# Moving one shift and one scaling of a layer norm between two matmul groups in a two-layer graph kernel

## The chip, the cores and the metric

The kernel runs on one core of one Trainium2 chip. The metric is device microseconds of one execution. A core has TensorE (matmuls, PE in the profile, with its weight loads as PEld), VectorE (DVE), ScalarE (ACT), GpSimd (POOL) and SyncE (SP), which here issues all DMA transfers.

## The reference

64 graphs of 256 nodes with 512 features, in two layers, all float32:

```python
# layer 0
deg = sum(adj, -1);  agg = (adj @ x) / max(deg, 1e-6)
x = layernorm(x + relu(concat([x, agg]) @ W.T))
# layer 1
q, k = split(x @ Wqk);  v = x @ Wv
agg = adj @ (k * mask)
w = mask * sum(q * agg, -1) / sqrt(512)
x = layernorm(x + softmax(w, over the nodes) * v)
```

The layer norm takes mean and variance over the 512 features of a node.

## The kernel before, in words

Graphs are worked on in 32 pairs. The main loop (`for j in range(NP)`) does layer 0 of pair j, and interleaves with its last third layer 1 of pair j-1, so that one round of the loop finishes one pair. A "graph" below is one of the two of a pair, k = 0 or 1; each has its 256 nodes in two tiles of 128, t = 0 and 1.

The matrix products are rearranged. Adjacency is applied after the feature weights, and the query and key weights are multiplied together once at the start. Each product of a 256x512 activation with a 512x512 weight is done in the Strassen-Winograd way: seven products P1 to P7 of blocks instead of eight, with sums of blocks prepared ahead. P1, P2, P3 and P5 are split once more in the same way inside (`inner`, L340), so each is four steps: `first_two`, `second`, `third`, `last_two`. P4, P6 and P7 are plain (`pairs`, L732, four units: two graphs with two halves each). `gather` (L405 on) is the product with the adjacency, with letters a to g.

The eight PSUM banks are used in four pairs. An `inner` product has a work bank (one half `lo`, one half `hi`) and a pair of target banks. Its steps follow this scheme: a matmul into `lo`, then ScalarE copies `lo` into a target bank, then the next step's matmul overwrites `lo`. In `third` ScalarE copies `lo` into both halves of the second target bank (128x512) and `hi` into a small tile, `fifth` (128x256). P5 of layer 0 and P3 of both layers share one work bank, P1 and P2 another. So a matmul of the next step or of the next product can start only when ScalarE has made its copy.

The order on every engine is the order in which the Python program emits instructions. The strings such as `run("p l p l p l", ...)` (L910) fix the order of TensorE by hand: each letter takes the next unit of a product. There p are the units of P4 of layer 1 and l the steps of P3 of layer 1 (`open1`); the last l and P3's end run in the next round (L795), between the first steps i of P1 and k of P5 of layer 0.

All other VectorE and ScalarE work is put into chains of steps (`queue`, L137): "norm" for the norm of layer 0, "softmax", "adds", "finish" for the norm of layer 1, "mask", "degrees", "sums". After most units `tick` (L152) goes through the chains by rank and emits a step when a planner's clock says so: the clock of TensorE goes forward by 0.43 or 0.86 us a matmul (`mm`, L174), each step has a cost and an estimated time at which its predecessor on another engine is done (L148). `flush` emits what is left of named chains. The planner decides only the order; on the chip, semaphores decide when.

The norm chain of a graph (`norm_of`, L478, called by `norm0`, L525) is: mean on VectorE (tile `less`), two squares with their sums on ScalarE (`junk`, `var`), the factor on ScalarE (`rstd`), the shift on VectorE (`shift` = `less` * `rstd`), and two scalings on ScalarE (`own` = `own` * `rstd` + `shift`), one for each tile. After the last one, a second chain of the same name holds two VectorE transposes (`turn`). A DMA then puts the pieces in place for the transposed activation of layer 1 (`places`, L798). Ahead of it, `send_scores` (L573) sends the scores of the pair before to DRAM and back, spread over all partitions for the softmax.

The scores themselves come from `dot` (L694): VectorE multiplies a bank of P4 (`u`) with the aggregated tile and sums it. The dot product of graph 0 follows the second unit p, that of graph 1 the fourth.

Of the kernel before, what the change touches and what calls it, by code (L numbers as in the profile page):

```python
# [94 lines left out]
def resnorm_kernel(  # L95
# [15 lines left out]
    NT, NF, NA = N // P, F // P, A // P  # L111
    H, HF = NF // 2, F // 2
    NP = B // 2
# [16 lines left out]
    clock, chains, shared, quiet = [0.0], [], [1.0], [False]  # L130
# [13 lines left out]
    def step(chain):  # L144
        _, name, ready, steps = chain
        eng, work = steps.popleft()
        work()
        ready[0] = eng.free + (0.4 if eng is not vec else 0.7 if name == "norm" and len(steps) == NT else 2.2 if name == "finish" or name == "norm" and steady else 1.4) if steps and steps[0][0] is not eng else 0.0  # L148
        if not steps:
            chains.remove(chain)  # L150
# [10 lines left out]
    def flush(*names):  # L161
        while True:
            c = next((c for c in chains if not names or c[1] in names), None)
            if not c:
                return
            step(c)

    def run(order, **units):
        for name in order.split():
            units[name].pop(0)()  # L170
# [31 lines left out]
    def load_xT(j, home=None):  # L202
        Xs[j] = Side(pool, "xT", S1, home)
        for k in range(2):
            first(Xs[j].a[:, k].rearrange("p h e t n -> p (h e) (t n)"),
                   x_t[2 * j + k].rearrange("(c p) n -> p c n", p=P))
# [78 lines left out]
    def fourth_sums(X, ks=(1, 0)):  # L285

        for k in ks:
            k = slice(k, k + 1)
            gp.tensor_sub(X.block(S4, k), X.block(A12, k), X.block(S2, k))
        if ks[-1] == 0:  # L290
            inner_sums(X, gp, 2)
# [27 lines left out]
    def mask_adj(j):  # L319
        def mask(k, t):  # L320
            act.activation(adjs[j][:, k, t], adjs[j][:, k, t], AF.Copy,
                           scale=mask_sb[:, 2 * j + k, t:t + 1])
        queue(4, "mask", *[(act, lambda k=k, t=t: mask(k, t)) for k in range(2) for t in range(NT)])

    def degrees(j):
        deg = small.tile([P, 2, NT], F32, name="deg")
        rdeg = rdegs[j] = small.tile([P, 2, NT], F32, name="rdeg")
        r = rows.pop(j)

        def degree(k, t):  # L330
            act.activation(r[:, k, t], r[:, k, t], AF.Copy, accum_out=deg[:, k, t:t + 1])

        def invert():
            vec.tensor_scalar(rdeg, deg, DEG_EPS, None, op0=OP.max)
            vec.reciprocal(rdeg, rdeg)
        queue(2, "degrees", *[(act, lambda k=k, t=t: degree(k, t)) for k in range(2) for t in range(NT)],
              (vec, invert))


    def inner(p, X, sides, w, q, done=lambda fifth: None):  # L340

        n, block = {"P1": (0, A11), "P2": (1, A12), "P5": (2, S1), "P3": (0, S4)}[p]
        b = sides[p]
        s = lambda r: X.i[:, r, n]
        lo, hi = w[:, :HF], w[:, HF:]
        fifth = []

        def first_two():
            mm(hi, s(0), b["T1"], start=True)
            mm(lo, X.chunk(block, 0, 0), b["B11"])  # L350
            act.copy(q[0][:, :HF], lo)
            tick()

        def second():
            mm(lo, s(1), b["T2"])
            act.copy(q[0][:, HF:], lo)
            tick()

        def third():
            mm(lo, s(2), b["T3"])  # L360
            act.copy(q[1].rearrange("p (h f) -> p h f", h=2),
                           lo[:, None, :].to_broadcast([P, 2, HF]))
            fifth.append(small.tile([P, HF], F32, name="fifth", bufs=3))
            act.copy(fifth[0], hi)
            mm(q[0][:, :HF], X.chunk(block, 0, 1), b["B21"])
            tick()

        def last_two():
            mm(q[1][:, :HF], X.chunk(block, 1, 1), b["T4"])
            mm(q[0][:, HF:], s(3), b["B22"])  # L370
            if p in ("P1", "P5"):
                for k in range(2):
                    vec.tensor_add(q[k][:, HF:], q[k][:, HF:], fifth[0])
            done(fifth[0])
            tick()
        return [first_two, second, third, last_two]
# [15 lines left out]
    def sums_T(val, later=None, n=3):  # L392

        b11, b12, b21, b22 = (val[:, :, t, h * HF:(h + 1) * HF] for t in range(NT) for h in range(2))
        tv = pool.tile([P, 4, 2, HF], F32, name="tv")
        t1, t2, t3, t4 = (tv[:, r] for r in range(4))
        vec.tensor_sub(t1, b12, b11)
        rest = [lambda args=args: vec.tensor_sub(*args) for args in ((t2, b22, t1), (t3, b22, b12), (t4, b21, t2))]
        for do in rest[:n]:
            do()  # L400
        if n < len(rest):
            later.extend(rest[n:])
        return {"B11": b11, "B21": b21, "B22": b22, "T1": t1, "T2": t2, "T3": t3, "T4": t4}
# [328 lines left out]
    def pairs(ps, X, slot, b, done):  # L732
        return outer(ps, 0, X, slot, b, done) + outer(ps, 1, X, slot, b, done)
# [23 lines left out]
    open1 = None  # L757
    early = []

    for j in range(NP):  # L760
        X = Xs.pop(j)
        if j == 2:
            steady.append(True)
        flush("finish")
        owns[j] = pool.tile([P, 2, NT, F], F32, name="own", bufs=3)
        if j > 0:
# [11 lines left out]
        p, q = pairs(u, X, S2, W0["T2"], a6), pairs(u, X, S3, W0["T3"], a7)  # L778
        r, s = inner("P3", X, W0, pw[1], y, a3), pairs(u, X, A22, W0["T4"], a4)
        if j == 0:  # L780
            run("i k i k i k i k", i=i, k=k)
            flush("degrees")
            load_rows(1)
        elif j == 1:
            early.append(a1)
            run("k i k m k i k", i=early[0], k=k, m=m)
            fourth_sums(X, [1])
            run("m p p", m=m, p=p)
            fourth_sums(X, [0])
            run("p p m", m=m, p=p)  # L790
            load_x(1)
        else:
            run("i k", i=i, k=k)
            send_scores(j - 2)
            run("i l k", i=i, k=k, l=open1)  # L795
            flush("norm")
            fetch_scores(j - 2)
            places[0](range(16))  # L798
            run("i k i k", i=i, k=k)
# [37 lines left out]
        def sums_next():  # L837
            if j == NP - 1:
                return
            inner_sums(Xs[j + 1], gp, 0)  # L840
            rest = outer_sums(Xs[j + 1], gp)
            run_now(rest[:1])
            inner_sums(Xs[j + 1], gp, 1)
            late_sums.extend(rest[1:])
# [42 lines left out]
        if j > 0:  # L887
            aggs[j - 1] = late.tile([P, 2 * N_SIDE], F32, name="agg").rearrange(
                "p (k t f) -> p k t f", k=2, t=NT)
            vs[j - 1] = [late.tile([P, NT, F], F32, name="v", bufs=2) for _ in range(2)]  # L890
            T = sums_T(owns[j - 1])
            g = gather(sumsM.pop(j - 1), T, aggs[j - 1], pw[0], o2[1], o2[0])
            h, q = pairs(u2, Y, S2, W1["T2"], b6), pairs(u2, Y, S3, W1["T3"], b7)
            n = inner("P5", Y, W1, pw[1], y2, b5)
            p, open1 = pairs(u2, Y, A22, W1["T4"], b4), inner("P3", Y, W1, pw[1], y2, b3)
            norm0(j)
            mask_adj(j)
            run("k h h" if j > 1 else "h h", k=k, h=h)
            if j == 1:
                degrees(2)  # L900
                flush("degrees")
            if j < NP - 1:
                load_xT(j + 1)
            run("n k h h" if j > 1 else "n h h", k=k, n=n, h=h)
            fourth_sums(Y)
            shared[0] = 1.25
            sums_next()
            run("a n b q d q n c q e q n p g f", n=n, q=q, p=p, **g)
            b8()
            run("p l p l p l", p=p, l=open1)  # L910
            py, pu = pu, py
        else:
            norm0(0)
            mask_adj(0)
            chains.extend(held)


    j = NP - 1
# [22 lines left out]
    p, r = pairs(u, X, A22, W1["T4"], b4), inner("P3", X, W1, pw[0], y, held.append)  # L941
# [87 lines left out]
```

## Time and profile before

Median of three runs: 1878.21 us (1877.14 to 1878.89). The profiled execution spans 1878.7 us at a TensorE clock of 0.998.

| what | value | how to read it |
|---|---|---|
| one round of the loop | 57.28 us, from 915.83 to 973.11 | between the first matmuls of layer 0's P1 in two rounds |
| ScalarE scalings `own<-own,shift,rstd` | 255 of 808 ns | of both norms |
| ScalarE squares `junk<-own,less` | 254 of 723 ns | of both norms |
| ScalarE copies bank to bank, 128x256 | 512 of 365 ns | each frees a half bank for a matmul |
| ScalarE copies bank to bank, 128x512 | 256 of 576 ns | the copy of `third` |
| ScalarE copies `fifth` | 256 of 377 ns | frees the other half |
| VectorE `turn` transposes | 120 of 686 ns | after the scalings |

A line of the timeline gives the start in us, the length, the engine, the program's line, the operation, what it writes and reads (without buffer numbers), the shape, and how many were merged into the line. Where the engine stood idle before, brackets give for how long and what ended it. All work that a helper emits carries the helper's line (L90 or L175), so one goes by tile names. A matmul of float32 is two records (two passes), with a weight load ahead of each.

### The profile page before, as it was taken

Reading aid. Unit: us, or ns where it says so; the run is one execution under the profiler, and the core shown is the slowest. Engines: PE = TensorE matmul, PEld = TensorE weight load, DVE = VectorE, ACT = ScalarE, POOL = GpSimd, SP = SyncE. Lnnn points to the kernel's source line nnn. Section 1 sums busy time; section 2 is a strip of 40 time slices with the busy share of each in tenths; the row PEclk is TensorE's granted clock in tenths of the full one; section 3 lists DMA queues with packets and bytes.
Section 4 is the critical chain, followed back from the end, with each engine's and each line's share of the span. In section 5 each row is a group of like instructions: output and inputs, shape, how many; then the busy total and the mean of one; then the engine's idle time right before and its main releaser. Section 6 shows DMA issues by size and latency. Waiting matters only on the chain.

```text
span 1878.7 us, 25017 instructions
## 1 busy us (share of the span) xinstructions
PE 1859.2 (99%) x7002; PEld 1312.9 (70%) x7002; DVE 1511.1 (80%) x3180; ACT 1308.7 (70%) x3274; POOL 909.6 (48%) x1255
## 2 busy tenths in 40 slices
PE   9999999999999999999999999999999999999997
PEld 5667767767777677677677777776776777776775
DVE  6787888777888778887778887788877788877887
ACT  3667776677777677767777776777676777767766
POOL 4455453555454554535554535554445544355532
PEclk9999999999999999999999999999999999999999
DMA  6133334333333433343333334333434333433321
GB/s 225 57 74 79 100 91 118 85 96 93 104 97 94 109 82 99 90 118 85 99 92 102 96 96 108 82 100 94 113 85 114 80 101 94 109 95 86 100 64 51
DMA packets 380714, 181.27 MB, mean 96 GB/s; under 512 B 263712, under 2 KB 345248, under 8 KB 380576
## 3 DMA queue, kind: packets, MB, share of 16 engines
q1 hardware_dynamic: 380576, 179.67, 35.8%
q8 instruction: 57, 0.93, 0.2%
q14 instruction: 81, 0.66, 0.1%
HBM read 114.10 MB, written 34.06 MB: 79 GB/s over the span
## 4 chain that ended last, share of the span: by engine, by line
PE 94%; POOL 2%; issue 2%; DVE 1%; ACT 1%; POOLq 0%; ACTq 0%; DVEq 0%
PE bank L175 94%; POOL xT_i L90 1%; ACT own L90 1%; POOL xT_s L90 0%; POOL sa L90 0%; DVE v L90 0%; DVE turn L90 0%; DVE own L90 0%; ACT bank L90 0%; ACT x1T L90 0%; DVE bank L90 0%; PE bank L629 0%; DVE st L90 0%; ACT adj L90 0%; PE bank L652 0%
## 5 line engine op out<-in xcount | busy, mean ns | idle before, releaser
L90 ACT COPY bank<-bank 128x256 f32<-128x256 f32 (+1 forms) x768 | 332.5, 435 | 234.9 <-PE bank L175 224.9
L90 DVE TENSOR_TENSOR y<-bank,y 128x512 f32<-128x512 f32 x256 | 170.4, 686 | 131.3 <-ACT y L90 130.7
L90 ACT ACTIVATE own<-own,shift,rstd 128x512 f32<-128x512 f32 x255 | 199.7, 808 | 0.9 <-DVE shift L90 0.9
L175 PE MATMUL bank<-tv,sa 128*128 128x256 f32 x768 | 192.5, 380 | 0.9 <-DVE tv L90 0.9
L90 POOL TENSOR_TENSOR x1T_s<-x1T,x1T_s 128x256 f32<-128x256 f32 x64 | 63.6, 1012 | 267.6 <-PE bank L175 267.6
L90 POOL TENSOR_TENSOR x1T_i<-x1T_s 128x128 f32<-128x128 f32 x128 | 101.1, 790 | 181.4 <-DVE x1T_s L90 181.4
L90 ACT ACTIVATE junk<-own,less 128x512 bf16<-128x512 f32 x254 | 183.7, 723 | 3.0 <-DVE less L90 2.0
L175 PEld LDWEIGHTS bank<-tv,sa 128*128 128x128 f32 x768 | 145.4, 190 | 49.6 <-issue 22.9
L90 ACT COPY y<-bank 128x512 f32<-128x512 f32 x192 | 108.7, 583 | 95.3 <-PE bank L175 93.8
L90 POOL TENSOR_TENSOR sa<-adj 128x256 f32<-128x256 f32 x128 | 93.7, 732 | 167.7 <-DMA adj<-adj_t 153.9
L175 PE MATMUL bank<-w,x1T_s 128*128 128x512 f32 (+1 forms) x384 | 168.3, 521 | 0.0
L90 POOL TENSOR_TENSOR x1T_i<-x1T 128x256 f32<-128x256 f32 x64 | 55.2, 863 | 224.9 <-DMA x1T<-turn 212.1
L175 PE MATMUL bank<-t,xT_s 128*128 128x512 f32 (+1 forms) x384 | 159.9, 526 | 2.6 <-ACT own L90 1.2
L90 DVE TENSOR_TENSOR v<-bank,v 128x512 f32<-128x512 f32 x186 | 119.1, 681 | 49.2 <-PE bank L175 49.2
L175 PE MATMUL bank<-t,x1T_s 128*128 128x512 f32 (+1 forms) x384 | 158.1, 521 | 0.3 <-ACT y L90 0.3
L175 PE MATMUL bank<-w,xT_s 128*128 128x512 f32 (+1 forms) x384 | 153.1, 521 | 0.0
L175 PE MATMUL bank<-t_i,xT_i 128*128 128x256 f32 x512 | 152.7, 380 | 0.3 <-POOL sa L90 0.2
L175 PE MATMUL bank<-t_i,x1T_i 128*128 128x256 f32 x512 | 152.2, 379 | 0.1
L175 PEld LDWEIGHTS bank<-t_i,x1T_i 128*128 128x128 f32 x512 | 97.1, 190 | 67.1 <-issue 49.5
L90 ACT COPY own<-bank 128x512 f32<-128x512 f32 x128 | 71.8, 587 | 92.1 <-PE bank L175 49.3
L175 PEld LDWEIGHTS bank<-t_i,xT_i 128*128 128x128 f32 x512 | 94.6, 189 | 58.2 <-issue 46.1
L175 PE MATMUL bank<-t,x1T 128*128 128x512 f32 x256 | 130.6, 592 | 0.0
(159 smaller groups left out, 4565.0 us busy)
## 6 DMA issues: line engine op xcount, KB each, us to landing
x<-x SPq DMA_DIRECT2D x64, 512.0 KB, 5.8
xT<-x_t SPq DMA_DIRECT2D x62, 512.0 KB, 5.7
out<-own SPq DMA_DIRECT2D x62, 512.0 KB, 3.3
x1T<-turn SPq DMA_DIRECT2D x480, 64.0 KB, 2.3
adj<-adj_t SPq DMA_DIRECT2D x64, 256.0 KB, 3.8
turn<-adj SPq DMA_DIRECT2D x64, 256.0 KB, 3.1
row<-d SPq DMA_DIRECT2D x31, 256.0 KB, 4.8
wqk<-wqk_t SPq DMA_DIRECT2D x4, 512.0 KB, 6.3
```

Source lines behind the costliest of these rows:

```text
L90: return self.tc.keep_in_program_order(getattr(self.engine, name)(out, *args, **kwargs))
L175: tc.keep_in_program_order(nc.tensor.matmul(ps, a, b, start=start, stop=True, skip_group_check=True))
```

## The change

In round j, after the third unit of P4 and the second step of P3, the norm chain of the graph that has exactly three steps left (its shift and two scalings) is stepped twice: the shift on VectorE and the first scaling on ScalarE are emitted there. The second graph's chain is the one in that state. The second scaling and the transposes stay with the planner. The purpose is to have the second graph's norm finished before the next round's first products, where its scalings and transposes stood. TensorE's order is not touched.

```diff
+    def hasten(name, left):
+        for c in list(chains):
+            if c[1] == name and len(c[3]) == left:
+                step(c)
+                step(c)
...
             b8()
-            run("p l p l p l", p=p, l=open1)
+            run("p l p l", p=p, l=open1)
+            if j < NP - 1:
+                hasten("norm", NT + 1)
+            run("p l", p=p, l=open1)
             py, pu = pu, py
```

`NT` is 2, the tiles of a graph, and `NP` is 32, the pairs. The condition leaves out the last round.

## The prediction

> **What bounds the kernel now.** I read the page first: engine busy time, the slices, the chain that ended last.
>
> ```profile
> PE 1859.2 (99%) x7002; PEld 1312.9 (70%) x7002; DVE 1511.1 (80%) x3180; ACT 1308.7 (70%) x3274; POOL 909.6 (48%) x1255
> PE   9999999999999999999999999999999999999997
> PEclk9999999999999999999999999999999999999999
> PE 94%; POOL 2%; issue 2%; DVE 1%; ACT 1%; POOLq 0%; ACTq 0%; DVEq 0%
> ```
>
> TensorE works through the whole span at full clock and 94% of the chain is its own. So only two things move the time: TensorE waits removed, and TensorE waits added. Its order of matmuls is the same before and after (compared in the compiled order), so I need only its gaps.
>
> Matmuls follow each other at a fixed beat: 128x256 starts 0.43 us after its predecessor (two passes), 128x512 0.86. Going through all 7002 records for starts later than the beat gives 21.8 us in all, and two places that repeat in each of 30 rounds (a round is one pass of the main loop, about 57.3 us). The first costs 5.8 us in total, the second 6.3 us. The first, in the timeline (start, length, engine, operation):
>
> ```profile
> 915.60 0.57 ACT L90 COPY bank<-bank 128x512 f32<-128x512 f32 x1 [0.93 <-PE bank L175]
> 916.08 0.38 ACT L90 COPY fifth<-bank 128x256 f32<-128x256 f32 x1
> 916.58 0.31 PEld L175 LDWEIGHTS bank<-t_i,xT_i 128*128 128x128 f32 x2
> 916.69 0.59 PE L175 MATMUL bank<-t_i,xT_i 128*128 128x256 f32 x2
> ...
> 918.02 0.81 ACT L90 ACTIVATE own<-own,shift,rstd 128x512 f32<-128x512 f32 x1
> 918.74 0.37 ACT L90 COPY bank<-bank 128x256 f32<-128x256 f32 x1
> 919.04 0.81 ACT L90 ACTIVATE own<-own,shift,rstd 128x512 f32<-128x512 f32 x1
> 919.76 0.84 ACT L90 COPY bank<-bank 128x256 f32<-128x256 f32 x2
> 920.24 0.30 PEld L175 LDWEIGHTS bank<-t,xT_i 128*128 128x128 f32 x2 [0.33 <-issue]
> 920.27 0.67 PE L175 MATMUL bank<-t,xT_i 128*128 128x256 f32 x2
> ```
>
> The two `own` scalings are those of the second graph. The second one holds up the copy at 919.76, and the matmul into the copied bank, due at 919.72 + 0.43 = 920.15, starts at 920.27; its second pass is another 0.07 late. Loss 0.19 us, 30 times. The weight load says what a wait costs: it starts 0.12 after the copy's end (919.76 + 0.36 = 920.12, 920.24), the matmul 0.03 later. See also the top: P5's first load at 916.58 is exactly 0.12 after `fifth` ends (916.46). It waits, yet the matmul at 916.69 is on the beat. That hand-over has no slack.
>
> The second place:
>
> ```profile
> 921.56 1.30 DVE L90 STREAM_TRANSPOSE turn<-own 128x512 f32<-128x512 f32 x2
> 922.78 1.39 DVE L90 TENSOR_TENSOR bank<-bank,fifth 128x256 f32<-128x256 f32 x4
> 923.22 1.07 ACT L90 COPY own<-bank 128x512 f32<-128x512 f32 x2 [1.38 <-DVE bank L90]
> 923.95 0.67 PE L175 MATMUL bank<-t,xT_s 128*128 128x512 f32 x1
> ```
>
> Two transposes hold VectorE, so four additions, two copies and a matmul come late: 0.21 us a round on average.
>
> **What the Trainium skill says.** "TensorE: Matmul & The Clock Gate", specification table: ScalarE and VectorE have strict FIFO queues. The trace agrees: at 919.04 a scaling nobody on TensorE needs goes ahead of a copy that TensorE waits for. "Perfetto Trace Analysis", section "Optimization Strategy", says to look for the gaps of the critical engine and for what it waits for; the 30 equal gaps are that. "PSUM — Partial Sum Buffer", section "Engine vs sequencer instructions": matmuls start and complete in program order, so one held matmul holds all behind it; the beat after 920.27 is shifted and not caught up. No page prices the two hand-overs; I take 0.12 and 0.03 from the trace.
>
> **The change part by part.** No instruction is added or removed in the arithmetic; the shift (0.15 us, VectorE) and the scalings (0.81 long; the next operation starts 0.72 after one, 918.02 to 918.74) move. I read the effect from the compiled order of the changed kernel.
>
> *Removed: first place.* Both scalings leave the stretch 918.0 to 919.8, and the copies there follow TensorE again. Gain 0.19 a round.
>
> *Removed: second place.* Three transposes instead of two now stand before the scores are sent, so one (0.69) instead of two stands before the four additions. They can begin up to 0.69 earlier, against 0.21 of loss. Gain 0.21. The scores leave 0.66 later, hidden: softmax's first exponential in the sample round runs some 10.9 us after the first P1 matmul (915.83), and its row lands at 7.6, at most 9.4 in the round I compared.
>
> *Added: a wait for `fifth`.* On ScalarE the order was copy, copy, copy of P3's third step, `fifth`. It becomes copy, copy, scaling, scaling, copy, `fifth`: the hastened step pulls the first scaling there, and the planner puts the second one directly behind it. The shift goes behind the first dot product, whose accumulator read begins at 914.38, so it ends at 914.53. The copy before runs 914.31 to 914.67 and its successor can begin about 0.1 before its end; so first scaling about 914.59, second 915.31, the 128x512 copy 916.03 instead of 915.60, `fifth` 0.48 later at 916.51 to 916.89, load 917.01, matmul 917.04 instead of 916.69. That is 0.35, and 0.07 for the slow second pass: 0.42 a round. The wait of ScalarE for the shift is not shown in the trace of before at this place; at least it costs nothing (0.40), at most 0.2 more (0.60). Behind the waiting matmul stands all of TensorE.
>
> *Added: a square before P3's second copy.* This doesn't show in the diff. The planner's clocks differ after the move, and on ScalarE the finish's first square now stands ahead of the second copy of the first layer's P3, in all 30 rounds. The round before:
>
> ```profile
> 933.25 0.58 ACT L90 COPY y<-bank 128x512 f32<-128x512 f32 x1 [0.50 <-PE bank L175]
> 933.73 0.38 ACT L90 COPY bank<-bank 128x256 f32<-128x256 f32 x1
> 933.91 1.03 PE L175 MATMUL bank<-w,xT_i 128*128 128x256 f32 x4
> 934.03 0.72 ACT L90 ACTIVATE junk<-own,less 128x512 bf16<-128x512 f32 x1
> ```
>
> The x4 are two matmuls; the second, due at 933.91 + 0.43 = 934.34, is P3's third step and writes the half bank that the copy at 933.73 reads until 934.11. Slack: 934.34 - 0.15 - 934.11 = 0.08. With the square first (its input `less` ends at 932.8 already and comes earlier in the new order) it takes 933.73; a square keeps the next ScalarE operation back by 0.70 (906.42 to 907.12 elsewhere in the trace), so the copy runs 934.43 to 934.81, load 934.93, matmul 934.96: 0.62 late, plus 0.07, so 0.69 a round. Lower end 0.55, if the two overlap more; upper end 0.75.
>
> *Other moves*: an exponential goes ahead of P2's second copy. That copy then ends near 11.8 us after P1's first matmul, and P2's third matmul, due at 12.04, needs 0.15; hidden by 0.1 to 0.2. Two squares leave the stretch of the first score copies, one scaling enters it before a copy with more than a microsecond to its reader. VectorE's additions and `less` come earlier. Order of DMA and of GpSimd is unchanged. I cost these at nothing.
>
> Sum: 0.42 + 0.69 - 0.19 - 0.21 = +0.71 a round; times 30 = +21.3 us. 1878.2 + 21.3 = 1899.5 us.
>
> **The rivals.**
> - *Only the gains count*: both new waits have slack that I don't see. For it: what moves away stands at both repeating gaps. Against it: the two hand-overs had 0.00 and 0.08 of slack. 1878.2 - 5.8 - 6.3 = 1866.1 us. Chance 0.06.
> - *Only one new wait bites.* With `fifth` alone 30 x (0.42 - 0.40) = +0.6, so 1878.8: no change. With the square alone 30 x (0.69 - 0.40) = +8.7, so 1886.9. Speaking for it: each of the two delays could be absorbed if ScalarE overlaps more. Against: the order of a strict queue is fixed. Chance 0.10, half of it each.
> - *The new waits and none of the second gain, or a third wait.* If VectorE's additions still come late, 30 x (0.42 + 0.69 - 0.19) = +27.6: 1905.8; with `fifth` at its upper end 30 x (0.60 + 0.69 - 0.19) = +33: 1911. For it: P2's second copy has little slack behind the exponential. Chance 0.10.
> - My forecast, 1899.5: 0.74.
>
> **How the numbers follow.** Lower ends of both new costs: 30 x (0.40 + 0.55 - 0.40) = 16.5, 1894.7; upper ends: 30 x (0.60 + 0.75 - 0.40) = 28.5, 1906.7. I widen to 1888 and 1909, so that of the rivals only the first two and the far end of the third are left out. Faster by over 0.2%: 0.07. Within 0.2% (`fifth` alone): 0.06. Slower: 0.87.
>
> **What would show it.** Right: TensorE gaps of some 0.4 before P5's first matmul and of some 0.7 before P3's third in each round, waiting for ScalarE; no gap left before P5's third and before P6; a round of about 58.0 us instead of 57.3; TensorE busy total hardly changed by arithmetic. Wrong: if `fifth` still ends 0.12 before P5's load on the beat, my timing of the shift fails; if P3's copy still follows `y`'s copy by half a microsecond and its matmul is on the beat, the square is cheaper than its row; a gap in a place not named above would mean I overlooked a moved instruction.

## The result and the profile after

The changed kernel takes 1908.01 us (median of four, 1907.01 to 1908.45), the kernel before 1878.55 us beside it (1877.14 to 1879.21). The ratio is 1.0157, 95% interval 1.0140 to 1.0175: slower by 29.5 us. The forecast was 1899.5, so the direction and the range held, and the loss was 8.2 us larger than the 21.3 us worked out. The profiled execution spans 1906.3 us against 1878.7, at the same clock of 0.998. That is a difference of 27.6 and not 29.5, because the profiled execution of the kernel before was one of its longer ones: it took 1880.45 us, 1.9 more than the median.

The page's busy times, and the shares of its chain of work by engine:

```profile
PE 1862.3 (98%) x7002; PEld 1318.2 (69%) x7002; DVE 1502.3 (79%) x3180; ACT 1309.5 (69%) x3274; POOL 905.4 (47%) x1255
...
PE 79%; DVE 8%; ACT 7%; issue 4%; POOL 1%; POOLq 0%; DVEq 0%; ACTq 0%
```

No engine has more work: ScalarE's 1309.5 us were 1308.7, TensorE's 1862.3 were 1859.2. The 40 slices of TensorE and of its clock read as before, digit for digit: 1.4 us in a round of 58 don't move a digit. What shows the loss is the chain: TensorE's share falls from 94% to 79%, and VectorE and ScalarE take up 15% together, where they had 2%. They now end waits that TensorE cannot get round.

I counted again how much later than the beat each of the 7002 matmul records starts. In all it is 50.3 us, where it was 22.5 by the same count (the prediction has 21.8). The difference, 27.8, is the difference of the spans, 27.6. By place, over 30 rounds, with both passes of the matmul that waits:

| place on TensorE | before, us | after, us | per round, after |
|---|---|---|---|
| before P5's third matmul | 5.8 | 0 | 0 |
| before P6 | 6.3 | 0 | 0 |
| before P5's first matmul (waits for `fifth`) | 0 | 19.7 | 0.66 |
| before P3's third matmul (waits for the copy behind the square) | 0 | 20.9 | 0.70 |

The four places that changed are the four that the prediction names. A round takes 58.17 us (928.33 to 986.50) where it took 57.28 and was forecast at 58.0. The first new wait, in the timeline of the kernel after:

```profile
926.27 0.69 DVE L90 SCALAR_TENSOR_TENSOR bank<-bank,agg 128x512 f32<-128x512 f32 x1
...
926.51 0.73 POOL L90 TENSOR_TENSOR sa<-adj 128x256 f32<-128x256 f32 x1 [1.33 <-DMA adj<-adj_t]
...
926.81 0.36 ACT L90 COPY bank<-bank 128x256 f32<-128x256 f32 x1 [0.93 <-PE bank L182]
...
926.88 0.36 DVE L90 TENSOR_TENSOR shift<-less,rstd 128x2 f32<-128x2 f32 x1
...
927.28 1.52 ACT L90 ACTIVATE own<-own,shift,rstd 128x512 f32<-128x512 f32 x2
...
928.76 0.59 PE L182 MATMUL bank<-w,xT 128*128 128x256 f32 x2
929.23 0.36 ACT L90 COPY fifth<-bank 128x256 f32<-128x256 f32 x1
...
929.70 0.30 PEld L182 LDWEIGHTS bank<-t_i,xT_i 128*128 128x128 f32 x2 [0.75 <-POOL sa L90]
929.73 0.67 PE L182 MATMUL bank<-t_i,xT_i 128*128 128x256 f32 x2 [0.38 <-ACT fifth L90]
```

Read it from the shift on. It is done at 926.88 + 0.36 = 927.24, the two scalings run from 927.28 without a break, and the 128x512 copy and `fifth` come behind them. `fifth` ends at 929.59, the weight load follows 0.11 later, the matmul 0.03 after that, where the beat asked for 928.76 + 0.43 = 929.19: 0.54 late, and its second pass 0.07 more. The load's own bracket names GpSimd's sums as releaser, but the last of them ends at 929.41 (928.69, 0.72 long), before `fifth`; the matmul's bracket has the right one.

The second new wait, P3 of the first layer in the same round:

```profile
946.42 0.72 ACT L90 ACTIVATE junk<-own,less 128x512 bf16<-128x512 f32 x1
...
946.60 0.59 PE L182 MATMUL bank<-w,xT_i 128*128 128x256 f32 x2
...
947.14 0.37 ACT L90 COPY bank<-bank 128x256 f32<-128x256 f32 x1
...
947.65 0.67 PE L182 MATMUL bank<-w,xT_i 128*128 128x256 f32 x2 [0.46 <-ACT bank L90]
```

Before, the copy into the bank stood directly behind that of `y`, where the square at 946.42 is now. It starts 0.72 later, at 947.14, and the matmul, due at 947.03, starts at 947.65.

The waits put the same in totals. The columns are total us, times and longest:

```profile
POOL sa L90 <- DMA adj<-adj_t: 40.9, 30, 1.6
...
PE bank L182 <- ACT bank L90: 14.1, 31, 0.5
...
PE bank L182 <- ACT fifth L90: 12.6, 30, 0.7
```

The last two are the new waits, less than the delays in the table because a matmul's wait is counted only from the end of the one before it, which lies after the beat. The first line was 153.9 us before, and I had not predicted that: GpSimd waits 113 us less for the adjacency of the next pair. This is the clue to the missing 8 us.

### The profile page after: what moved, and what is told of

Read it like the earlier page. It is cut to its first block, busy times and chain, and to the rows that moved or that the text cites. A ratio compares the mean times of both kernels' runs of the same rounds, so it can differ in the third digit from the quotient of the medians.

```text
span 1906.3 us, 24928 instructions
## 1 busy us (share of the span) xinstructions
PE 1862.3 (98%) x7002; PEld 1318.2 (69%) x7002; DVE 1502.3 (79%) x3180; ACT 1309.5 (69%) x3274; POOL 905.4 (47%) x1255
## 4 chain that ended last, share of the span: by engine, by line
PE 79%; DVE 8%; ACT 7%; issue 4%; POOL 1%; POOLq 0%; DVEq 0%; ACTq 0%
PE bank L182 79%; DVE v L90 3%; ACT own L90 3%; DVE bank L90 2%; ACT bank L90 1%; ACT junk L90 1%; DVE y L90 1%; DVE agg L90 1%; ACT y L90 1%; POOL xT_i L90 1%; DVE own L90 1%; ACT fifth L90 1%; DVE shift L90 0%; POOL xT_s L90 0%; POOL sa L90 0%
## 5 line engine op out<-in xcount | busy, mean ns | idle before, releaser
L90 POOL TENSOR_TENSOR xT_s<-xT,xT_s 128x256 f32<-128x256 f32 x62 | 45.1, 729 | 187.4 <-PE bank L182 187.4
L182 PE MATMUL bank<-w,xT_i 128*128 128x256 f32 x384 | 116.5, 385 | 14.1 <-ACT bank L90 14.1
```

The lines of the kernel that those rows point to most:

```text
L90: return self.tc.keep_in_program_order(getattr(self.engine, name)(out, *args, **kwargs))
L182: tc.keep_in_program_order(nc.tensor.matmul(ps, a, b, start=start, stop=True, skip_group_check=True))
```

## The experiments

Ratios are to the kernel before, run beside them: its median was 1879.46 us beside the first four kernels, 1878.79 beside the other four.

### One suspect each: the square, and what remains

The first two start from the changed kernel. One keeps the whole finish where it was before the change, by silencing the planner over the two units ahead of P3's second copy (q, the last unit of P7, and r, the second step of P3):

```diff
-        run("r q r m", m=m, q=q, r=r)
+        run("r", r=r)
+        hold = quiet[0]
+        quiet[0] = j > 1
+        run("q r", q=q, r=r)
+        quiet[0] = hold
+        run("m", m=m)
```

> The changed kernel, with the planner kept from emitting chain steps from the first layer's seventh product until P3's second copy, so that the finish's squares, and with them its scalings, output and the next adjacency load, stand where they stood before the change. Theory: the wait before P3's third matmul (0.70 us a round) goes, and since the adjacency sums no longer run on GpSimd while the hastened shift runs, the wait before P5's first matmul falls from 0.66 to about 0.42. With both old gaps still away: 1878.6 + 30 x (0.42 - 0.40) = 1879 us, within 2 us. Rival, that the wait before P5 is the two scalings alone and GpSimd has no part in it: 0.66 stays, 1878.6 + 30 x (0.66 - 0.40) = 1886 us.

Measured: 1881.49 us, ratio 1.0009 (1.0000 to 1.0018): 2.0 us above the kernel before beside it, where about 0.6 was expected. The profiled span is 1878.6. The wait at P3 is gone, that at P5 remains, and both old gaps stay away.

The other lets the rest of the finish come as early as in the changed kernel, and only puts the first square of graph 0 behind P3's second copy:

```diff
-        run("r q r m", m=m, q=q, r=r)
+        run("r", r=r)
+        if j > 1:
+            barred.append("finish")
+        run("q r", q=q, r=r)
+        if j > 1:
+            hasten("finish", 6, 1)
+        run("m", m=m)
+        barred.clear()
```

(`tick` skips chains whose name is in `barred`; the third argument of `hasten` is the number of steps.)

> The changed kernel, with only the finish's first square of graph 0 put back behind P3's second copy; the scalings of the finish, the output and the adjacency load stay early. Theory: the wait before P3's third matmul goes (30 x 0.70 = 21 us less: 1887 us), the wait before P5's first matmul stays at 0.66 a round, since the shift still meets the adjacency sums. Rival, that the wait at P3 only moves to the next copy or matmul: between 1890 and 1908 us.

Measured: 1886.57 us, ratio 1.0038 (1.0023 to 1.0052). Again no wait at P3, so moving that one square accounts for it. But the two kernels, which should cost the same if `fifth` is the only wait left, differ by 5.1 us. Their timelines differ at P5: 12.8 us of late starts with the finish held, 18.8 with it early. The kernel with the finish held:

```profile
913.48 0.36 ACT L90 COPY bank<-bank 128x256 f32<-128x256 f32 x1 [0.93 <-PE bank L182]
...
913.55 0.15 DVE L90 TENSOR_TENSOR shift<-less,rstd 128x2 f32<-128x2 f32 x1
913.75 1.52 ACT L90 ACTIVATE own<-own,shift,rstd 128x512 f32<-128x512 f32 x2
...
915.43 0.59 PE L182 MATMUL bank<-w,xT 128*128 128x256 f32 x2
...
916.20 0.67 PE L182 MATMUL bank<-t_i,xT_i 128*128 128x256 f32 x2 [0.17 <-ACT fifth L90]
```

Here the shift takes 0.15, ScalarE's first scaling starts 0.27 after the copy before it, and the matmul is 0.34 late. In the kernel after the shift takes 0.36 and the scaling starts 0.47 after the copy. Over 29 rounds (the first with a moved shift is left out) its median is 0.150 with the finish held (0.148 to 0.152), 0.402 with it early (0.148 to 0.633), and 0.39 (0.25 to 0.68) in the kernel after.

What stretches a 128x2 product from 0.15 to 0.68? In the round shown it ends at 927.24, and GpSimd's sum `sa` at 926.51 + 0.73 = 927.24. In each of the 29 rounds the shift ends 0.01 to 0.02 after the sum. The Trainium skill, "SBUF — State Buffer", section "Who interferes with whom", states that a VectorE instruction with two SBUF inputs contends with a GpSimd instruction that reads SBUF, and that the one that comes second is blocked for the whole instruction. The shift is such an instruction (`less` and `rstd`), and the traces agree, with 0.15 against 0.25 to 0.68. The kernel with only the square put back shows both cases: in four of its rounds no sum runs yet when the shift starts, the shift takes 0.15, and P5's first matmul is 0.34 to 0.35 late, as with the finish held. The dot product at 926.27, which has one of its inputs in PSUM, overlaps the same sum, and neither is stretched: it takes 0.69 and the sum 0.73. Before the change the sum wasn't there. The first of GpSimd's sums of that round, in the timeline of the kernel before:

```profile
918.08 0.73 POOL L90 TENSOR_TENSOR sa<-adj 128x256 f32<-128x256 f32 x1 [5.40 <-DMA adj<-adj_t]
```

Counted from the round's first P1 matmul (915.83 and 928.33), it starts at +2.25 there and at -1.82 in the kernel after (926.51). The reason is SyncE's queue: the adjacency load stands behind the finish's output there. The queue in the kernel before, and then in the kernel after:

```profile
912.89 0.38 SPq L180 DMA_DIRECT2D out<-own  x1
913.38 1.33 SPq L180 DMA_DIRECT2D adj<-adj_t  x2
```

```profile
909.89 0.38 SPq L187 DMA_DIRECT2D out<-own  x1
922.93 0.88 SPq L187 DMA_DIRECT2D adj<-adj_t  x2
```

Before, the load is issued directly behind the output, 2.45 ahead of the round's first P1 matmul. The change makes the finish earlier, the output has long gone out, and the load is issued 5.40 ahead. With the finish held the sums are late again, at +3.65 (918.65 against 915.00), and GpSimd's wait for adjacency is 155.4 us, close to the 153.9 before.

Round by round the delay follows the shift. In the 29 rounds of the kernel after, the shift's length and the late start of P5's first matmul (without its second pass) have a correlation of 1.0 (rounded): the shortest shift, 0.251, goes with 0.427 us, the longest, 0.680, with 0.858.

### The square alone

On the kernel before, nothing but the square moved ahead of P3's second copy:

```diff
-        run("r q r m", m=m, q=q, r=r)
+        run("r q", q=q, r=r)
+        if j > 1:
+            ahead("finish", 6)
+        run("r m", m=m, r=r)
```

> The kernel before, with only the finish's first square put ahead of P3's second copy; shift and scalings stay where they were. Theory: a wait of 0.70 us a round before P3's third matmul, 30 x 0.70 = 21 us more: 1899.5 us, within 2 us. Rival, that the square costs this only because the hastened scaling pushed other work of ScalarE against it: 1879 us.

Measured: 1899.89 us, ratio 1.0110 (1.0095 to 1.0125). Late starts at P3 are 20.9 us, as many as in the changed kernel, in the same line of the waits:

```profile
PE bank L181 <- ACT bank L90: 14.1, 31, 0.5
```

So a single moved instruction, which the diff doesn't mention, is worth 0.70 us a round by itself.

### The sums taken away from the shift

If the shift is stretched by GpSimd's sums, then moving these, in the changed kernel and with the finish left early, must bring it back to 0.15. The four sums are emitted after `fourth_sums(X, [0])` here. They start 13.2 us after the round's first P1 matmul, 15 us later than in the kernel after:

```diff
-            sumsA[j] = adj_sums(j)
+            if j == 1:
+                sumsA[j] = adj_sums(j)
...
+            if j > 0:
+                sumsA[j] = adj_sums(j)
```

> The changed kernel, with GpSimd's sums of adjacency blocks for layer 0 emitted behind the second product's sums, some 12 us later in the round; the load of the adjacency stays early. ScalarE's and VectorE's order is that of the changed kernel. Theory: the shift, which now ends 0.02 us after a GpSimd sum ends, is free and takes 0.15 us again, the wait before P5's first matmul falls from 0.66 to about 0.42: 30 x 0.24 = 7 us less, 1901 us. Rival, that the slow shift comes from the accumulator read before it: no change, 1908 us.

Measured: 1901.21 us, ratio 1.0116 (1.0101 to 1.0131). At the place in dispute the answer is plain: the shift is 0.149 (0.148 to 0.151), and P5's first matmul loses 12.7 us instead of 19.7. That the total also came out as expected is partly chance. At their new place the sums collide with VectorE's weighted additions of the second layer, which have two SBUF inputs as well (`v` and `own`):

```profile
938.86 1.30 DVE L90 SCALAR_TENSOR_TENSOR own<-v,probs,own 128x512 f32<-128x512 f32 x1
938.89 0.73 POOL L90 TENSOR_TENSOR sa<-sa,adj 128x256 f32<-128x256 f32 x1
...
939.58 1.18 POOL L90 TENSOR_TENSOR sa<-adj 128x256 f32<-128x256 f32 x1
...
940.10 1.20 DVE L90 SCALAR_TENSOR_TENSOR own<-v,probs,own 128x512 f32<-128x512 f32 x1
...
940.71 1.18 POOL L90 TENSOR_TENSOR sa<-adj,sa 128x256 f32<-128x256 f32 x1
...
941.23 0.68 DVE L90 TENSOR_TENSOR y<-bank,y 128x512 f32<-128x512 f32 x1
...
941.90 0.74 DVE L90 SCALAR_TENSOR_TENSOR own<-v,probs,own 128x512 f32<-128x512 f32 x1
...
942.50 0.67 PE L182 MATMUL bank<-t_i,xT_i 128*128 128x256 f32 x2 [0.26 <-ACT bank L90]
```

Both sides are stretched, 1.30 and 1.20 where the one after the sums takes 0.74, and 1.18 where the sum before took 0.73. The ends show them taking turns: a sum ends at 939.62, an addition at 940.16, a sum at 940.76, an addition at 941.30, a sum at 941.89. The addition `y<-bank,y` at 941.23 has one input in PSUM, runs beside the last sum and takes 0.68 as elsewhere. It and the `less` behind it come late, so ScalarE's copies do, and P3's second matmul loses 15.0 us. As TensorE then reaches P3's third matmul later, that wait shrinks from 20.9 to 6.2, by 14.7. The sum of these two changes of opposite sign happened to be small.

### The same idea with other places

The gains at the two old gaps are real. Can they be had without the waits? Here the norm's pieces are spread over places at which the copy behind them has slack: the shift before the dot products that `b8` emits, one scaling after P4's second unit and P3's first step, the other after P4's third unit and P3's second step. The diff is against the changed kernel.

```diff
+            if j < NP - 1:
+                barred.append("norm")
+                hasten("norm", NT + 1, 1)
             b8()
-            run("p l p l", p=p, l=open1)
+            run("p l", p=p, l=open1)
+            if j < NP - 1:
+                hasten("norm", NT, 1)
+            run("p l", p=p, l=open1)
             if j < NP - 1:
-                hasten("norm", NT + 1)
+                hasten("norm", NT - 1, 1)
+            barred.clear()
             run("p l", p=p, l=open1)
```

With these places alone, the square still ahead of P3's copy:

> As the kernel before in this list, but with the finish's square ahead of P3's second copy, as in the changed kernel. Theory: only the wait before P3's third matmul stays: 1867 + 30 x 0.70 = 1888 us, within 2 us; no wait before P5's first matmul. Rival, that fifth is late for another reason than the scalings ahead of it: 1907 us.

Measured: 1888.40 us, ratio 1.0051 (1.0037 to 1.0065). Only P3's 20.9 us are left as a repeating delay. With the square put behind the copy too, by the edit shown above:

> The changed kernel with the three steps of graph 1's norm spread over gaps of their engines: the shift before the dot products, the first scaling behind P3's first copy, the second behind P3's second copy, so that the 128x512 copy and fifth aren't late; and the finish's square behind P3's second copy. The finish stays early. Theory: both new waits go and both old gaps stay away: 1879 - 12 = 1867 us, within 2 us. Rival, that the old gaps were only filled by the new waits and come back in another place when these go: 1879 us or more.

Measured: 1867.74 us, ratio 0.9940 (0.9928 to 0.9953). This beats both kernels, the one before by 11 us and the changed one by 40. No repeating gap is left, 9.6 us of late starts remain in the whole span, and the shares of the chain by engine say so:

```profile
PE 96%; issue 1%; POOL 1%; ACT 1%; DVE 0%; POOLq 0%; DVEq 0%; ACTq 0%
```

In the timeline one can see why the places work:

```profile
904.12 1.28 POOL L90 TENSOR_TENSOR xT_s<-xT 128x512 f32<-128x512 f32 x1
...
905.08 0.34 DVE L90 TENSOR_TENSOR shift<-less,rstd 128x2 f32<-128x2 f32 x1
...
905.72 0.36 ACT L90 COPY bank<-bank 128x256 f32<-128x256 f32 x1 [1.56 <-PE bank L186]
...
905.99 0.82 ACT L90 ACTIVATE own<-own,shift,rstd 128x512 f32<-128x512 f32 x1
...
907.01 0.36 ACT L90 COPY bank<-bank 128x256 f32<-128x256 f32 x1 [0.20 <-PE bank L186]
...
907.28 0.81 ACT L90 ACTIVATE own<-own,shift,rstd 128x512 f32<-128x512 f32 x1
...
908.30 0.57 ACT L90 COPY bank<-bank 128x512 f32<-128x512 f32 x1 [0.20 <-PE bank L186]
```

After each single scaling ScalarE idles for 0.20 until TensorE comes, so the scaling fills idle time and makes no copy wait. And the shift is stretched here too (0.34, ending 0.02 after another of GpSimd's sums), but it ends 0.57 before the scaling that reads it starts.

The same places with the finish held instead of the square put back:

> The three steps of graph 1's norm in the gaps of their engines as in the first of this list, and the planner kept quiet around P3's second copy, so that the finish with output and adjacency load stands as in the kernel before. Theory: 1867 us as in the first, the early finish is worth nothing by itself. Rival, that the early finish is what removes the old gap before P6: about 1873 us.

Measured: 1868.08 us, ratio 0.9943 (0.9929 to 0.9957). The same, so whether the finish is early or late is worth nothing once neither the shift nor P3's copy stands in its way.

### A cheaper repair that missed

The last one leaves shift and first scaling where the change put them, and moves only the second scaling to the next round, behind P5's first copy. At that place, I reckoned, it delays no copy:

```diff
             if j < NP - 1:
                 hasten("norm", NT + 1)
+                barred.append(1)
...
+            hasten("norm", NT - 1, 1)
+            barred.clear()
```

(Here `barred` holds the rank of the chains that the planner passes over.)

> The changed kernel with only graph 1's second scaling put later, behind P5's first copy; the hastened shift and first scaling stay. The planner then leaves the finish where it was before the change, and two transposes stand after the scores again. Theory: one scaling ahead of the 128x512 copy costs nothing, since ScalarE stands idle there for 0.93 us, so fifth is in time; the old gap before P5's third matmul stays away (5.8 us), the old gap before P6 comes back with the two transposes: 1879 - 6 = 1873 us, within 2 us. Rival, that any scaling between P3's second and third copy makes fifth late: 1879 us or more.

Measured: 1878.53 us, ratio 0.9998 (0.9990 to 1.0006): no change, 5 us more than expected. The delays at P5's first and third matmul are gone as expected. But the gap before P6 grew from 6.3 to 9.7 us:

```profile
918.65 1.30 DVE L90 STREAM_TRANSPOSE turn<-own 128x512 f32<-128x512 f32 x2
...
919.87 1.40 DVE L90 TENSOR_TENSOR bank<-bank,fifth 128x256 f32<-128x256 f32 x4
...
921.04 1.96 PE L186 MATMUL bank<-t,xT_s 128*128 128x512 f32 x4
```

The two transposes still hold up the four additions, as before the change. TensorE, no longer late at P5, reaches P6 earlier and waits there for what it saved: the gain of 5.8 us gives 3.4 back. The profiled span is 1875.9 us, 2.8 below the one before, but the timed runs don't show that much: the execution profiled here took 0.9 us less than its median, that of the kernel before 1.9 more.

## Why the prediction came out as it did

*What bounds the kernel.* Right. The time lost is the sum of TensorE's late starts, 27.8 against 27.6 us of span, with the order of matmuls unchanged.

*Removed: first place, 0.19, and second place, 0.21.* Right, both gone entirely. The prediction has the second gap in each of 30 rounds; it is in 21 of them, and the total of 6.3 us is right. The kernel with other places shows their worth: 1867.74 against 1878.79 beside it, 11.1 us for the 12.1 that the two gaps summed to. So the rival "only the gains count" (1866.1) is the kernel that this change could have been.

*Added: a square before P3's second copy, 0.69.* Right: 0.70, alone (1899.89), and nothing when put back. Its cause is in the trace as forecast: a strict queue, a bank free 0.72 later, 0.08 of slack.

*Added: a wait for `fifth`, 0.42.* The mechanism was right, the size was off. It measured 0.66. This is the mis-sized term of the sum: 30 x 0.24 = 7.2 of the 8.2 us missing. My range for the term, 0.40 to 0.60, did not reach it. Of the rest 0.3 us is P3's 0.70, and 0.7 lies within the spread of the runs before (1877.14 to 1879.21).

What failed in it is the step that the shift "ends at 914.53", with a length of 0.15 that was taken from the trace of before, and behind that the sentence "Order of DMA and of GpSimd is unchanged. I cost these at nothing." The order was unchanged. The time was not: the load of the adjacency stands behind the finish's output in SyncE's queue, the finish came earlier for the same reason as the square, and so GpSimd's sums came over 4 us earlier and lay on the shift. With the sums away, by two different edits, the wait was 0.42 to 0.43, exactly as worked out; with them there, 0.63 to 0.66. That settles the cause of the size. That the block is the shared read port is the page's mechanism; the runs show the coincidence of the ends and the stretching in turns, which fit it. A kernel in which the shift reads one input only wasn't tried, but the trace of the kernel after has other instructions of both kinds. The addition `y<-bank,y`, with one input in PSUM, has a median of 0.69 us both away from GpSimd's sums (140 times) and beside one for over half its length (72 times); `own<-own,x`, with both in SBUF, has 0.69 away from them (32) and 1.10 beside them (96). The number of SBUF inputs is not the whole of it, though: `less<-sum` has one such input and a constant, and is stretched as well, from 0.16 to a median of 0.45.

*Other moves, costed at nothing.* The exponential ahead of P2's copy, the score copies and the later row of the softmax cost nothing indeed: no further repeating gap is in the trace.

*The rivals.* `fifth` alone was forecast at 1878.8 and measured, by holding the finish, at 1881.49 (beside a kernel before at 1879.46, so +2.0 against +0.6). The square without the wait for `fifth` was forecast at 1886.9; the kernel with other places and the early square took 1888.40. Against the kernels before beside them, these two had the right prices to within 2 us; both waits simply occurred at once. The third rival, 1905.8 to 1911, has the measured time inside it, nearer than the forecast, but not for its reason: the second gain came in full and no third wait appeared. What its upper variant shares with the measurement is a longer wait for `fifth`, 0.60 there and 0.66 measured. And that the range held is in part luck: the upper ends of the two terms added up to 1906.7, and 1908.01 lies inside only because the range was widened to 1909.

## What to carry to other kernels

When an instruction is moved on an in-order engine, work out what slack the *next* operation there has to its reader on the critical engine: 0.08 us of slack and a 0.72 us instruction in front of it cost 0.70 us a round. With a planner, compare the compiled order of all engines, since half of the waiting that the change added, 20.9 of 40.6 us, came from an instruction that the diff never named. And an unchanged order is not an unchanged time: follow what comes earlier through the DMA queue to what it will now lie beside, and don't take the length of a short VectorE instruction from a place where GpSimd was idle.

## What the runs showed that was not expected

- A VectorE product of 128x2 with two SBUF inputs takes 0.15 us alone and up to 0.68 beside a GpSimd sum, and ends within 0.02 us of the sum's end. On VectorE's long operations the same meeting cost 0.46 to 0.56 us each (1.20 and 1.30 against 0.74), and GpSimd's sum became 1.18 instead of 0.73, because the two engines took turns. A VectorE addition with one input in PSUM kept its 0.69.
- A delay taken away upstream can come back downstream: 3.4 of 5.8 us did, when another engine's lateness at the next place hadn't been taken away with it.
